# Pinned statistics and scalings in the later projections, and diagonal taps on TensorE in the last causal convolution

## The chip, the cores and the metric

The kernel runs on one core of a Trainium2 chip. The core has five engines with a queue each: TensorE (PE, matmuls), VectorE (DVE), ScalarE (ACT), GpSimd (POOL) and SyncE (SP), which only starts transfers here. The metric is the device time of one execution in microseconds (us); the median of three runs before the change is 3825.23 us. The profile is one execution of the same program, recorded by the hardware.

## The reference

The input is x of shape (4, 512, 128, 64): 4 batch entries, T = 512 time steps and D = 128 x 64 = 8192 features. All arithmetic is 32-bit float. Two layers follow each other.

Layer 0, for each batch entry:

1. Layer norm over D, then three projections to 64 columns, `k = xn @ Wk`, `v = xn @ Wv`, `r = sigmoid(xn @ Wr)`. A recurrence over time, `s = decay * s + k * v`, gives the states; `x = x + (r * states) @ Wo`.
2. Layer norm; a convolution with three taps along the 128 frequencies that mixes the 64 channels; GELU; added to x.
3. Layer norm; a *causal* depthwise convolution along time, three taps for each feature: `to[t] = w2 * xn[t] + w1 * xn[t-1] + w0 * xn[t-2] + bias`; layer norm of the result; added to x.
4. A feed-forward network, 64 channels to 256, GELU, back to 64; added to x.

Layer 1 is a spectral filter along time (moving average as trend, discrete Fourier transform of the rest, 128 modes mixed by complex matrices, inverse transform). The change does not touch it.

## The kernel before

**Tiling.** In layer 0 the 8192 features lie on the partitions in 64 chunks of 128, with the 512 time steps along the free axis. Chunks are handled in 32 pairs, so most tiles are 128 x 2 x 512. A layer norm over D is folded into the work: sums of x and of its squares come from matmuls against ones (`add_up`, L251), a few small operations give one factor and one offset for each time step, and `rows` spreads them over all partitions (L241 on TensorE, L285 on ScalarE).

**Stages**, for each batch entry b:

- `project(b)`: the three projections. Each pair of chunks needs the transposed x (`load_x`), a pair of weights, and for the first layer norm also x with time on the partitions (`xk`), from which VectorE takes `bn_stats` (L354). VectorE multiplies the weights by the norm's gain in place (L370), and TensorE accumulates over all chunks (L373).
- `scan(b)`: a short chain with the recurrence.
- `attend_and_convolve(b)`: `Wo` (L495), the addition to x (L497), normalising (L501), the frequency convolution (L516, L525, L530), GELU (L531), the residual (L533), squares (L536) and sums (L251) for the next norm.
- `convolve_time(b)`: the causal convolution. `normed` makes the normalised x in two VectorE operations (L569, L572); `tapped` makes one tap and the bias on ScalarE (L577) and adds the two others on VectorE (L581), chunk by chunk; GpSimd mends the first two time steps (L587) and stores (L588); ScalarE squares (L628). `convolve_ahead(b)` does 14 of the 32 pairs earlier, for b = 1 and 2.
- `open_feed(b)`, `feed_forward(b)`: for each pair the last norm and residual (L647, L648, L656, L659); for each chunk `widen` (L679, GELU L683), `narrow` (L690, residual L695) and `store` (transposes L704, copies L711 and L713, GpSimd's store L715).

**What sets the order.** TensorE's instructions stand in the order of the program. The list in `in_turn` pairs the stages: each entry gives two lanes of work, of which one step at a time is taken so that both advance by their shares. The entries that matter are feed-forward 0 beside projection 2, feed-forward 1 beside projection 3, and feed-forward 2 beside the causal convolution of b = 3, the last one. `begin` and `needed` hold a lane back until what it reads exists. On the other engines the framework's scheduler chooses the order from priorities and its own estimates, except for instructions marked by `tc.keep_in_program_order`, which keep the program's order among themselves and around them. Before the change, in projections 2 and 3 (`b > 1`), only the first of the two statistics of a pair is marked; the second and the scalings are placed by the scheduler.

**Buffers.** `xk` for `b > 1` lies alternately in the tags `x2` and `sq`, two buffers each; two pairs' weights share one `wx` buffer, of which there are two; `load_x` has three. `narrow` has a single PSUM bank, tag `p`, so L690 of a chunk waits for L695 of the chunk before. In the last convolution the sums lie in one of the two banks of the tile `a`, and the other is unused. SP's queue issues the loads of `project`, `normed` and `residual`; GpSimd's queue issues the stores.

Of the kernel before, what the change touches and what calls it, by code (L numbers as in the profile page):

```python
# [79 lines left out]
def layer0(ctx, tc, dram, x, xt, vecs, wkvr, wo, wdec, wconv, fbias, w1, fb1, w2, fb2, x4):  # L80
# [241 lines left out]
    def project(b):  # L322
# [5 lines left out]
        for i in range(NPR):  # L328
            first, last = i == 0, i == NPR - 1
            if unscanned[0]:  # L330

                wq, xk = two(fr, "x1")[:, :, 0 : 4 * S + 3], spare("z", SL)
            elif b == 1:

                both = spare("wx", 4 * S + SL)
                wq, xk = both[:, :, 0 : 4 * S], both[:, :, 4 * S :]
            else:

                xk = two(bk, "sq" if i % 2 else "x2")
                if i % 2 == 0:  # L340
                    pairs = spare("wx", 4 * S + SL).rearrange("p k n -> p (k n)")[:, 0 : 16 * S]
                    pairs = pairs.rearrange("p (c s) -> p c s", c=4)
                    nc.sync.dma_start(pairs, wkvr[2 * i : 2 * i + 4, :, 0 : 4 * S].rearrange("c p s -> p c s"))
                wq = pairs[:, i % 2 * 2 : i % 2 * 2 + 2, :]
            if b < 2:
                n = 4 * S + 2 * (b == 0)
                nc.sync.dma_start(wq[:, :, 0 : n], wkvr[2 * i : 2 * i + 2, :, 0 : n].rearrange("c p s -> p c s"))
            xp = load_x(b, i)
# [3 lines left out]
            )  # L352
            for t in range(2):
                stats = nc.vector.bn_stats(stt[:, h + t, s, :], xk[:, t, :])  # L354
                if b > 1 and t == 0:

                    tc.keep_in_program_order(stats)
            if b == 0:
# [9 lines left out]
            for j in range(2):  # L368
                w = wq[:, j, 0 : 3 * S]
                nc.vector.tensor_scalar_mul(w, w, vec[:, G1, 2 * i + j : 2 * i + j + 1])  # L370
# [108 lines left out]
    def attend_and_convolve(b):  # L479
        rst, rs, mrs = scanned.pop(b)  # L480
        rb, mb = yield from rows(of_a, rs, mrs, "rm")

        nc.vector.tensor_scalar(mb, mb, at_one[:, 1:2], at_one[:, 0:1], ALU.mult, ALU.add)
        st = ps_s.tile([P, SL], F32, tag="s", name="st")
        free_s[0] = False
# [58 lines left out]
        for i in range(2):  # L544
            scaled(i)
        for i in range(NPR + 3):
            if i < NPR:
                attend(i)
                yield 1.0
            if 1 < i < NPR + 2:  # L550
                convolve(i - 2)
                yield 5.0
            if i > 2:
                add_up(st, i - 3, *waiting.pop(i - 3), i == 3, i == NPR + 2)
                yield 1.0
        begin[attend_and_convolve], free_s[0] = b + 1, True
# [542 lines left out]
```

## Time and profile before

| what | value |
|---|---|
| median of three runs | 3825.23 us (3824.32 to 3826.63) |
| the profiled execution's own time | 3829.78 us |
| its span, first to last instruction | 3828.0 us |
| mean granted TensorE clock | 0.981 |
| VectorE taps, L581, x512 | 372.2 us busy, 0.74 us each |
| VectorE scalings, L370, x256 | 71.7 us busy, 0.31 to 0.32 us each |
| ScalarE tap and bias, L577, x256 | 200.1 us busy, 0.80 to 0.81 us each |

The page gives each engine's busy time as a share of the span and then groups of instructions by line: `L690 PE MATMUL pa<-mid,w_sb ... x2048` reads as line 690, TensorE, a matmul that writes tile `pa` from `mid` and `w_sb`, 2048 records. One 32-bit matmul leaves two records. Busy time of matmuls overlaps, because they are pipelined. "Idle before" is what the engine stood still just ahead of that group, with the instruction that ended it; idle time of an engine that is not the bound costs nothing. The stages follow each other: projection 0 to about 157 us; attention 0 beside projection 1 to 521; causal convolution 0 beside attention 1 to 810; feed-forward 0 beside projection 2 to 1264; convolution 1 beside attention 2 to 1510; feed-forward 1 beside projection 3 to 1927; convolution 2 beside attention 3 to 2174; feed-forward 2 beside convolution 3 to 2518; feed-forward 3 to 2831; layer 1 to the end.

### The profile page before, as it was taken

The page shows a single profiled execution, that of the slowest core. Times are in us where ns is not written, and L with a number is a line of the kernel's source. Part 1 is how long each engine was busy: PE and PEld are TensorE (multiplying, and loading weights), DVE is VectorE, ACT ScalarE, POOL GpSimd, SP SyncE. Part 2 cuts the span into 40 slices and gives each one's busy share as a digit, 9 for nine tenths or more (in the row PEclk, how much of TensorE's full clock was granted, in tenths as well). Part 3 has the DMA queues.
Part 4 walks back from the last instruction along what each step waited for, and adds up shares of the span by engine and source line. Part 5 has one row for each costly group of instructions (what it writes and reads, how often), then busy time and mean ns, then how long its engine had stood idle before and what let it go on. Part 6 is the DMA issues. An engine that isn't in the chain of part 4 may idle for free. (4 is left out here: it accounts for less than half of the span.)

```text
span 3828.0 us, 44882 instructions
## 1 busy us (share of the span) xinstructions
PE 3626.8 (95%) x15945; PEld 1344.1 (35%) x15945; DVE 2680.8 (70%) x3498; ACT 1762.2 (46%) x2491; POOL 510.8 (13%) x782
## 2 busy tenths in 40 slices
PE   9999999989899899999989989999989999999999
PEld 4433322233333223333322323333322843327533
DVE  4455569975667796677789699855558268892677
ACT  0022346645556565556756578867754210142100
POOL 0000012210011221011121121100013001121001
PEclk9999999999999999999989999999999999999999
DMA  9867657786775687777568677645559468994687
GB/s 311 267 210 247 217 171 254 262 276 228 250 250 195 215 281 270 261 262 278 203 233 284 215 247 256 218 155 176 187 197 283 145 215 295 313 307 145 200 289 271
DMA packets 429175, 912.80 MB, mean 238 GB/s; under 512 B 33240, under 2 KB 83608, under 8 KB 424856
## 3 DMA queue, kind: packets, MB, share of 16 engines
q1 hardware_dynamic: 351024, 636.87, 50.2%
q0 software_dynamic: 75776, 271.62, 20.4%
q8 instruction: 127, 2.08, 0.2%
q10 hardware_dynamic: 2152, 1.45, 0.1%
q14 instruction: 96, 0.79, 0.1%
HBM read 641.31 MB, written 268.50 MB: 238 GB/s over the span
## 5 line engine op out<-in xcount | busy, mean ns | idle before, releaser
L690 PE MATMUL pa<-mid,w_sb 128*64 128x512 f32 x2048 | 500.6, 610 | 56.5 <-DVE x4t L695 56.4
L683 ACT ACTIVATE mid<-m,fb_sb 128x1024 f32<-128x1024 f32 x256 | 284.9, 1113 | 264.4 <-PE m L679 264.1
L695 DVE SCALAR_TENSOR_TENSOR x4t<-pa,fb_sb,x 128x512 f32<-128x512 f32 x252 | 187.4, 744 | 225.1 <-PE pa L690 225.1
L679 PE MATMUL m<-x,w_sb 64*128 64x512 f32 x1008 | 289.4, 647 | 1.1 <-DVE x L659 0.7
L683 ACT ACTIVATE mid<-c,fb_sb 128x1024 f32<-128x1024 f32 x256 | 283.1, 1106 | 1.4 <-PE c L679 1.4
L679 PE MATMUL c<-x,w_sb 64*128 64x512 f32 x1008 | 264.1, 597 | 9.8 <-ACT mid L683 9.8
L690 PEld LDWEIGHTS pa<-mid,w_sb 128*64 128x64 f32 x2048 | 125.2, 137 | 401.4 <-issue 216.4
L373 PE MATMUL a<-xp,wx 128*128 128x512 f32 x512 | 243.0, 601 | 0.5 <-DVE me L268 0.5
L967 PE MATMUL b<-xin,avg_sb 128*128 128x512 f32 x512 | 230.8, 593 | 3.3 <-DVE xin L973 3.3
L944 ACT COPY two<-a 128x512 f32<-128x512 f32 x64 | 37.5, 585 | 425.2 <-PE a L939 425.2
L973 DVE TENSOR_TENSOR xin<-b,pm 128x512 f32<-128x512 f32 x256 | 158.9, 682 | 96.6 <-PE b L970 81.7
L536 ACT ACTIVATE sq<-x 128x1024 f32<-128x1024 f32 x128 | 135.0, 1055 | 179.8 <-DVE x L533 178.5
L581 DVE SCALAR_TENSOR_TENSOR to<-kd,vec,to 128x510 f32<-128x510 f32 (+1 forms) x272 | 196.8, 741 | 16.7 <-ACT to L577 11.0
L656 ACT ACTIVATE kd<-kd,vec 128x512 f32<-128x512 f32 x256 | 193.4, 809 | 4.1 <-DVE kd L648 4.1
L849 DVE COPY xf<-b 128x256 f32<-128x256 f32 x128 | 54.3, 424 | 185.0 <-PE b L913 173.3
L704 PEld LDWEIGHTS pt<-ident,x4t 128*128 128x128 f32 x1024 | 107.7, 141 | 208.5 <-ACT mid L683 141.2
L251 PE MATMUL st<-x,ones 128*32 128x512 f32 x512 | 168.3, 604 | 12.2 <-DVE x L533 12.1
L581 DVE SCALAR_TENSOR_TENSOR z<-x,vec,z 128x511 f32<-128x511 f32 x240 | 175.4, 743 | 5.2 <-ACT z L577 2.3
L870 DVE TENSOR_TENSOR uv<-xin 128x1024 f32<-128x1024 f32 x128 | 154.9, 1228 | 33.0 <-PE a L879 16.4
L495 PE MATMUL a<-rst,wo_sb 64*128 64x512 f32 x512 | 149.9, 660 | 28.7 <-DVE x L497 26.0
L497 DVE TENSOR_TENSOR x<-a,xp 128x1024 f32<-128x1024 f32 x128 | 155.9, 1218 | 27.0 <-PE a L495 24.3
L704 PE MATMUL pt<-ident,x4t 128*128 128x128 f32 x1024 | 168.7, 288 | 1.5 <-ACT ob L711 1.5
(241 smaller groups left out, 6513.4 us busy)
## 6 DMA issues: line engine op xcount, KB each, us to landing
xp<-in_xt SPq DMA_DIRECT2D x256, 512.0 KB
xin<-x SPq DMA_DIRECT2D x128, 1024.0 KB
kh<-to SPq DMA_DIRECT2D x156, 512.0 KB
x<-x POOLq DMA_DIRECT2D x128, 512.0 KB, 4.7
kx<-x SPq DMA_DIRECT2D x128, 512.0 KB
x<-ob POOLq DMA_DIRECT2D x64, 1024.0 KB, 6.1
out<-xin POOLq DMA_DIRECT2D x64, 1024.0 KB, 7.2
x<-x SPq DMA_DIRECT2D x96, 512.0 KB
```

The lines of the kernel that those rows point to most:

```text
L251: nc.tensor.matmul(st[32 * q : 32 * q + 32, :], lhsT=ones, rhs=src[:, j, :], start=first, stop=last,)
L373: nc.tensor.matmul(pa[:, k, :], lhsT=wq[:, j, k * P : (k + 1) * P], rhs=xp[:, j, :], start=first and j == 0, stop=last and j == 1,)
L497: nc.vector.tensor_tensor(x1, at, xp, ALU.add)
L581: tap = nc.vector.scalar_tensor_tensor(to[:, j, k:], xr[:, j, : SL - k], vec[:, w, c], to[:, j, k:], ALU.mult, ALU.add)
L656: tc.keep_in_program_order(nc.scalar.activation(d[:, j, :], d[:, j, :], AF.Identity, bias=vec[:, B4, c], scale=vec[:, G4, c]))
L679: nc.tensor.matmul(pm[:, h, :], lhsT=w1_sb[hs, m * P : (m + 1) * P], rhs=x3[hs, :], start=True, stop=True)
L683: nc.scalar.activation(mid, pm, AF.Gelu_apprx_tanh, bias=fb1_sb[:, m : m + 1])
L690: nc.tensor.matmul(pa[h * H : (h + 1) * H, :], lhsT=w2_sb[:, m, :], rhs=mid[:, h, :], start=(m == 0), stop=(m == 1),)
L695: nc.vector.scalar_tensor_tensor(x4t, pa, fb2_sb, x3s[c // 2][:, c % 2, :], ALU.add, ALU.add)
L704: nc.tensor.transpose(pt[:, t, :], x4t[:, t * P : (t + 1) * P], ident)
L967: nc.tensor.matmul(po[j], lhsT=avg_sb[:, j, :], rhs=xin[:, j, :], start=True, stop=False)
L973: nc.vector.tensor_tensor(by_n(xin[:, j, :]), by_n(po[j]), by_c(pm[j % 2][:, j // 2, :]), ALU.add)
```

## The change

It has three parts.

1. **Projections 2 and 3** (`project`, `b > 1`). Both statistics of a pair and both scalings are marked to keep the program's order. In the program the load of `xk` for pair i is issued at step i, and its statistics are taken at step i + 2; the weights are loaded for the two pairs after the current ones; `load_x` runs one pair ahead. The order within a step is: loads, the statistics of pair i - 2, the scalings of pair i, the matmuls of pair i.
2. **Attention 1's start.** A lane can now yield `BLOCKED` from inside a stage. Instead of waiting for the end of attention 0, attention 1 makes its rows at once (in buffers of their own, `rm4`) and may take its first three steps while attention 0's last ones are still under way. The PSUM bank for its sums is taken only at its fourth step.
3. **The last causal convolution** (`tapped` with `left`). In every other pair the second chunk gets all three taps on TensorE: GpSimd multiplies the identity by the three tap weights of the chunk, which gives three diagonal 128 x 128 matrices; three matmuls of 512, 511 and 510 columns add up in the unused bank of `a`; ScalarE adds the bias while it copies to SBUF. There are 16 such chunks of the 64. They need none of the two VectorE taps.

```diff
@@ -325,36 +325,60 @@
         if b == 0:
             psum_w = ps_p.tile([P, SL], F32, tag="p", name="psum_w")
         stt = rowp.tile([P, NT, NS, 6], F32, tag="stt", name="stt")
-        for i in range(NPR):
-            first, last = i == 0, i == NPR - 1
-            if unscanned[0]:
-
-                wq, xk = two(fr, "x1")[:, :, 0 : 4 * S + 3], spare("z", SL)
-            elif b == 1:
-
-                both = spare("wx", 4 * S + SL)
-                wq, xk = both[:, :, 0 : 4 * S], both[:, :, 4 * S :]
-            else:
-
-                xk = two(bk, "sq" if i % 2 else "x2")
-                if i % 2 == 0:
-                    pairs = spare("wx", 4 * S + SL).rearrange("p k n -> p (k n)")[:, 0 : 16 * S]
-                    pairs = pairs.rearrange("p (c s) -> p c s", c=4)
-                    nc.sync.dma_start(pairs, wkvr[2 * i : 2 * i + 4, :, 0 : 4 * S].rearrange("c p s -> p c s"))
-                wq = pairs[:, i % 2 * 2 : i % 2 * 2 + 2, :]
-            if b < 2:
-                n = 4 * S + 2 * (b == 0)
-                nc.sync.dma_start(wq[:, :, 0 : n], wkvr[2 * i : 2 * i + 2, :, 0 : n].rearrange("c p s -> p c s"))
-            xp = load_x(b, i)
+        def token_major(i, xk):
             s, h = i // 2, i % 2 * 2
             nc.sync.dma_start(
                 xk, x[b, h * P : (h + 2) * P, s * SL : (s + 1) * SL].rearrange("(t p) d -> p t d", p=P)
             )
+            return xk
+
+        def statistics(i, xk):
+            s, h = i // 2, i % 2 * 2
             for t in range(2):
                 stats = nc.vector.bn_stats(stt[:, h + t, s, :], xk[:, t, :])
-                if b > 1 and t == 0:
+                if b > 1:
 
                     tc.keep_in_program_order(stats)
+
+        def weights(i):
+
+            if i < NPR:
+                w = spare("wx", 4 * S + SL).rearrange("p k n -> p (k n)")[:, 0 : 16 * S]
+                w = w.rearrange("p (c s) -> p c s", c=4)
+                nc.sync.dma_start(w, wkvr[2 * i : 2 * i + 4, :, 0 : 4 * S].rearrange("c p s -> p c s"))
+                for k in range(2):
+                    ws[i + k] = w[:, 2 * k : 2 * k + 2, :]
+
+        ws, xps, xks = {}, {}, {}
+        if b > 1:
+            weights(0)
+            xps[0] = load_x(b, 0)
+        for i in range(NPR):
+            first, last = i == 0, i == NPR - 1
+            if b > 1:
+
+
+                xks[i] = token_major(i, two(bk, "sq" if i % 2 else "x2"))
+                if i % 2 == 0:
+                    weights(i + 2)
+                if not last:
+                    xps[i + 1] = load_x(b, i + 1)
+                wq, xp = ws.pop(i), xps.pop(i)
+                for k in (i - 2, NPR - 2, NPR - 1) if last else (i - 2,):
+                    if k in xks:
+                        statistics(k, xks.pop(k))
+            else:
+                if unscanned[0]:
+
+                    wq, xk = two(fr, "x1")[:, :, 0 : 4 * S + 3], spare("z", SL)
+                else:
+
+                    both = spare("wx", 4 * S + SL)
+                    wq, xk = both[:, :, 0 : 4 * S], both[:, :, 4 * S :]
+                n = 4 * S + 2 * (b == 0)
+                nc.sync.dma_start(wq[:, :, 0 : n], wkvr[2 * i : 2 * i + 2, :, 0 : n].rearrange("c p s -> p c s"))
+                xp = load_x(b, i)
+                statistics(i, token_major(i, xk))
             if b == 0:
                 nc.gpsimd.memset(wq[:, :, n:], 1.0)
                 for j in range(2):
@@ -367,7 +391,9 @@
                     )
             for j in range(2):
                 w = wq[:, j, 0 : 3 * S]
-                nc.vector.tensor_scalar_mul(w, w, vec[:, G1, 2 * i + j : 2 * i + j + 1])
+                scaled = nc.vector.tensor_scalar_mul(w, w, vec[:, G1, 2 * i + j : 2 * i + j + 1])
+                if b > 1:
+                    tc.keep_in_program_order(scaled)
             for j in range(2):
                 for k in range(2):
                     nc.tensor.matmul(
@@ -478,11 +504,9 @@
 
     def attend_and_convolve(b):
         rst, rs, mrs = scanned.pop(b)
-        rb, mb = yield from rows(of_a, rs, mrs, "rm")
+        rb, mb = yield from rows(of_a, rs, mrs, "rm4" if b == 1 else "rm")
 
         nc.vector.tensor_scalar(mb, mb, at_one[:, 1:2], at_one[:, 0:1], ALU.mult, ALU.add)
-        st = ps_s.tile([P, SL], F32, tag="s", name="st")
-        free_s[0] = False
         x1s, zs, ws, waiting = {}, {}, {}, {}
 
         def attend(i):
@@ -541,18 +565,26 @@
                 scaled(i + 2)
             waiting[i] = x2, sq2
 
-        for i in range(2):
-            scaled(i)
         for i in range(NPR + 3):
+
+            while begin[attend_and_convolve] < b + (min(i, 3) - 3) / 4:
+                yield BLOCKED
+            if i < 2:
+                scaled(i)
             if i < NPR:
                 attend(i)
                 yield 1.0
             if 1 < i < NPR + 2:
                 convolve(i - 2)
                 yield 5.0
+            if i == 3:
+                st = ps_s.tile([P, SL], F32, tag="s", name="st")
+                free_s[0] = False
             if i > 2:
                 add_up(st, i - 3, *waiting.pop(i - 3), i == 3, i == NPR + 2)
                 yield 1.0
+            if b == 0 and i >= NPR and i < NPR + 2:
+                begin[attend_and_convolve] = b + (0.25 if i == NPR else 0.75)
         begin[attend_and_convolve], free_s[0] = b + 1, True
         mean3, sq3 = yield from finish(st, of_a, 3)
         carried[b] = moments(mean3, sq3, 3)
@@ -571,9 +603,24 @@
             tc.keep_in_program_order(first)
         nc.vector.tensor_tensor(xr, xr, pair_of(mb), ALU.subtract)
 
-    def tapped(b, i, xr, to, pinned=False):
+    def tapped(b, i, xr, to, pinned=False, left=None):
+
         for j in range(2):
             c = slice(2 * i + j, 2 * i + j + 1)
+            if j == 1 and left is not None:
+                taps = fr.tile([P, 2, P + H], F32, tag="wcs", name="taps").rearrange("p k n -> p (k n)")
+                taps = taps.rearrange("p (k n) -> p k n", k=3)
+                nc.gpsimd.tensor_tensor(
+                    taps, ident.unsqueeze(1).to_broadcast([P, 3, P]),
+                    vec[:, W0 : W2 + 1, c].to_broadcast([P, 3, P]), ALU.mult,
+                )
+                for k in range(3):
+                    nc.tensor.matmul(
+                        left[:, k:], lhsT=taps[:, 2 - k, :], rhs=xr[:, j, : SL - k], start=k == 0, stop=k == 2,
+                        skip_group_check=True,
+                    )
+                nc.scalar.activation(to[:, j, :], left, AF.Identity, bias=tb_all[:, c])
+                continue
             nc.scalar.activation(
                 to[:, j, :], xr[:, j, :], AF.Identity, bias=tb_all[:, c], scale=vec[:, W2, c]
             )
@@ -607,7 +654,11 @@
             rb, mb = ahead.pop(b)
         else:
             rb, mb = yield from rows(bank, *moment, "rm" if b == B - 1 else "rm3")
-        st = bank()
+        if b == B - 1:
+            both = two(ps_a, "a")
+            st, left = both[:, 0, :], both[:, 1, :]
+        else:
+            st, left = bank(), None
         waiting, added = [], 0
         n = NPR - made
         for k in range(n + 2):
@@ -624,7 +675,7 @@
                     sq = bk.tile([P, 2, SL], F32, tag="sq4", name="sq4", bufs=2)
 
                 normed(b, made + k, x2, xr, rb, mb, made > 0 and k < 4)
-                tapped(b, made + k, xr, to)
+                tapped(b, made + k, xr, to, left=left if k % 2 else None)
                 nc.scalar.activation(sq, to, AF.Square)
                 waiting.append((k, to, sq))
                 i = k * made // n
@@ -740,11 +791,12 @@
 
 
     CHAIN = 6.0
+    BLOCKED = -1.0
 
     def run(b, stages):
         for stage, share in stages:
             for weight in stage(b):
-                yield weight * share / whole[stage]
+                yield BLOCKED if weight == BLOCKED else weight * share / whole[stage]
 
     def in_turn(leads, *pairs):
         at, running = [0.0, 0.0], [None, None]
@@ -754,10 +806,12 @@
             b, *stages = pairs[n][k]
             if running[k] is None:
                 first = stages[0][0]
-                if first in needed and b not in needed[first] or begin.get(first, b) < b:
+                if first in needed and b not in needed[first]:
                     return False
                 running[k] = run(b, stages)
             share = next(running[k], None)
+            if share == BLOCKED:
+                return False
             if share is None:
                 running[k] = None
                 at[k] = n + 1.0
```

## The prediction

> **What bounds the kernel now.** I read the page's engine totals first, then busy times by stretch, then the waits and the order of time inside two stretches. The stretches, by busy time of each engine (start and end in us, then each engine's busy us and count, the granted clock, the DMA share and GB/s):
>
> ```profile
> PE 3626.8 (95%) x15945; PEld 1344.1 (35%) x15945; DVE 2680.8 (70%) x3498; ACT 1762.2 (46%) x2491; POOL 510.8 (13%) x782
> ...
> 902.50:1173.30 270.80, 247.54 (x961) 88.93 (x960) 180.27 (x242) 149.22 (x201) 25.47 (x30) 1.00 0.73 249
> 1644.90:1864.80 219.90, 219.28 (x865) 80.75 (x864) 161.36 (x213) 133.28 (x181) 22.86 (x27) 1.00 0.78 271
> 2190.00:2470.00 280.00, 245.91 (x1192) 81.93 (x1192) 272.89 (x310) 233.79 (x310) 58.94 (x75) 0.98 0.72 242
> ```
>
> TensorE is the bound almost everywhere. The first stretch (feed-forward 0 beside projection 2) leaves it idle for 23 us. The second (feed-forward 1 beside projection 3) leaves it nothing: 9 equal cycles of four chunks take 219.9 us, 24.4 us each. The first stretch holds 10 such cycles, 27.1 us each. The third (feed-forward 2 beside the last causal convolution) is VectorE's: 272.9 of 280 us. Its waits, and those of the first stretch (who waited for whom, us in total, times, longest):
>
> ```profile
> DVE stt L354 <- DMA sq<-in_x: 54.8, 9, 7.0
> DVE stt L354 <- DMA x<-in_x: 27.6, 9, 3.2
> ...
> PE pa L690 <- DVE x4t L695: 32.8, 26, 3.9
> ```
>
> The first two lines are VectorE held up by the statistics' loads, in the first stretch; the third is TensorE waiting for VectorE, in the last. In order of time (start, us, line):
>
> ```profile
> 1003.77 0.68 DVE L354 BATCH_NORM_STATS2 stt<-sq 128x6 f32<-128x512 f32 x1
> 1011.45 0.69 DVE L354 BATCH_NORM_STATS2 stt<-sq 128x6 f32<-128x512 f32 x1 [7.00 <-DMA sq<-in_x]
> 1012.06 0.73 DVE L695 SCALAR_TENSOR_TENSOR x4t<-pa,fb_sb,x 128x512 f32<-128x512 f32 x1
> 1012.71 1.22 DVE L569 TENSOR_TENSOR x<-x,rm 128x1024 f32<-128x1024 f32 x1
> 1012.85 1.94 PE L690 MATMUL pa<-mid,w_sb 128*64 128x512 f32 x8 [1.78 <-DVE x4t L695]
> ...
> 1715.30 1.94 PE L690 MATMUL pa<-mid,w_sb 128*64 128x512 f32 x8
> 1717.17 0.66 PE L704 MATMUL pt<-ident,x4t 128*128 128x128 f32 x4
> 1717.29 0.75 DVE L695 SCALAR_TENSOR_TENSOR x4t<-pa,fb_sb,x 128x512 f32<-128x512 f32 x1 [3.06 <-PE pa L690]
> 1717.66 1.88 PE L373 MATMUL a<-xp,wx 128*128 128x512 f32 x4
> ```
>
> A statistic waits 7 us for a load that could start only when the statistic before it (1003.77) freed the buffer; the residual L695 queues behind it, and TensorE stands 1.78 us. Below, in cycle 2, the order that matters: narrow matmuls L690, transposes L704 0.49 us long, then the projection's matmuls L373. L695 starts only 0.12 us after the transposes, because it needs the end of L690.
>
> **What the skill says.** TensorE: Matmul & The Clock Gate, "Step-by-step: what each phase is for": matmuls stay in program order, only weight loads are pulled ahead. Its specification table gives the other engines strict first-in-first-out queues. The trace agrees: L690 at 1012.85 holds all behind it, and L695 stands behind the late statistic. Perfetto Trace Analysis, "Identifying the Most-Contended Engine", warns that matmul busy time is no measure of the roofline; so I use start-to-start steps.
>
> **Part 1, projections 2 and 3.** The loads move ahead: weights by two pairs, the transposed x by one, and the statistics run two pairs after their load. So each load is issued a cycle or so before its use, nothing new can block in SP's queue, and VectorE's DMA waits (54.8 + 27.6 = 82 us in the first stretch) should go. But all statistics and scalings are now pinned in program order. In the built program VectorE's order before was, per four chunks, residual, taps, four scalings in one go, drawn one to two pairs ahead, and L373 waited for no scaling. After, each pair reads: L695, statistic, statistic, scaling, scaling; and on TensorE the first L373 of the pair stands right behind L690 and the transposes. So it must wait for L695 (which needs that very L690), two statistics and one scaling. Loads that waited cost VectorE slack; this wait is TensorE's own.
>
> Steps from start to start in the traces above: L690 1.87, L704 0.49, L373 1.80, L679 0.96 and 0.95: 6.07 a chunk, 24.3 a cycle. VectorE: L695 0.66, statistic 0.61, scaling 0.31 to its end (0.23 to the next), 1024-wide operations 1.14 (1.25 when the next reads the result), taps 0.66. From VectorE's end to the matmul 0.06, and 0.1 more because the weights load after it (estimate from projection 0, where such pairs are 0.53 instead of 0.43 apart).
>
> Cycle in stretch 1, t=0 at the transposes. One pair has the short chain: 0.12 + 0.66 + 1.22 + 0.31 + 0.16 = 2.47 against 0.49 due: 1.98 us stall. For the other, VectorE is still busy with the normalising, residual and tap work that stands between: 0.12 + L695 0.66 + five 1024-wide 5.8 + two taps 1.32, then L695 0.66, 1.22, 0.31, 0.16: 10.25. TensorE would be there at 6.07 + 0.49 = 6.56: 3.7 us stall. The cycle is 24.3 + 5.7 = 29.95, against 27.1 now.
>
> Cycle in stretch 2: two pairs' statistics and scalings come in two bursts, behind two residuals, N (L569), X (L659), n (L572): 0.12 + 0.66 + 3.4 + 1.22 + 0.31 + 0.16 = 5.87 against 0.49: 5.4 us stall for one pair; the other's weights are ready. 24.3 + 5.4 = 29.7 against 24.4 now.
>
> Sum by the built order. Projection 2: four early pairs at 2.0 = 8; 10 cycles x 2.8 = 28; a half cycle 3.7 and a last pair behind six statistics (2.0 + 4 x 0.61 = 4.4) = 8: +44. Projection 3: four early 8, one cycle of the first kind 5.7, nine of the second 48.6, the last with four more statistics 7.8: 70, less some 5 us of stalls by late loads that go: +65. If VectorE reached each scaling by the time the transposes end, the cost would be nothing; the cover needed is a scaling ahead of L695, and the built order has none.
>
> **Part 2, attention 1 begins in attention 0's tail.** Its two row spreads and first matmuls move before the last sums. Around 500 to 550 us TensorE waits 7.6 us in pieces for rows, x and sums; I take -3 (0 to -5).
>
> **Part 3, taps on TensorE.** Removed: 32 VectorE taps x 0.74 = 23.7 us; 16 ScalarE scalings become copies with bias (0.80 before; evictions of this size take 0.59: no cost). Added: 48 matmuls of 128x512, two records 0.43 apart each: 0.86 x 48 = 41 us of TensorE; 16 diagonals of 384 columns on GpSimd. No trace shows those; GPSIMD Engine Reference, "3.1 Elementwise", states about 2.6 cycles an element: an estimate of 0.8 us, plus the 0.7 to 0.9 that even a 4-wide one takes here: 1.5. GpSimd builds them three pairs ahead, so TensorE shouldn't wait; the following square on ScalarE may come 0.5 us later. Queued behind that square are ScalarE's GELUs: 0 to 0.7 us a time, 16 times. The normalised x stands well ahead of the matmul in VectorE's order. In 2190 to 2470 TensorE does 48 chunks x 4.36 (the alone stage's step: 240 us for 55) + 28 sums x 1.0 = 237 us, to the 246 that show as busy. Plus 41: 279 to 288, plus 5 to 15 of stalls, against 280. From -1 to +23; I take +8. VectorE's 249 of 288 no longer binds.
>
> Total: 44 + 65 - 3 + 8 = +114. The profiled execution took 3829.78 (span 3828.0 and 1.8 around it), 4.6 over the median 3825.23; so 3944 profiled, **3939 us** as median.
>
> **Rivals.** (a) Short waits only: VectorE catches up and every affected pair costs 2.0. Projection 2: early 8, ten cycles at 28.3 (+12), tail 7: +27. Projection 3: 8, ten cycles +40, tail 2, less 5: +45. With +5: 3902. Against it: nothing in VectorE's order can overtake. (b) The diagonal path is worse: the square and GELU queue costs 2 us in each of 16 pairs, +32: 3971. For it: four engines in one chain there; against it: diagonals are ready early. (c) Faster: scalings are never late, and the DMA waits were the true cost: stretch 1 falls to 24.4 a cycle, 10 x 2.7 = -27, seam -3, taps 0: 3795. It decides when the mean wait of the 64 pairs stays under (27 + 3)/64 = 0.47 us; the shortest chain alone is 1.98. (d) Nothing measurable: gains of part 1 meet part 3's loss, 3825; it needs the same as (c).
>
> **Numbers.** Main 0.70, (a) 0.13, (b) 0.11, (c) 0.04, (d) 0.02. Its own range, with the taps at -1 to +23 and a tenth of part 1's 109 either way, is 3919 to 3965. To leave no more than 2 in 10 out I take 3892 (a, with the taps at -1) to 3974. A change under 0.2% (7.6 us) can't be told from none here: faster 0.04, same 0.02, slower 0.94.
>
> **What would show it.** Right: L373 idle before some 42 of 64 pairs with the scaling (L370 before) as releaser, 2 to 5.4 us each, 73 + 70 = 143 us by the sums above (57 + 16 and 70); four-chunk cycles near 30 us in both projections; no statistic waiting for a load; the last convolution's stage with VectorE near 86% and about as long as now. Wrong: L373 without such waits, because matmul and scaling stand otherwise than I read; or a last stage grown by over 25 us, with TensorE waiting for GpSimd or ScalarE.

## The result and the profile after

The changed kernel takes **4021.2 us** (median of 4 runs, 4016.38 to 4029.38), the kernel before, run beside it, 3824.78 us: ratio 1.052, 95% interval 1.0496 to 1.0543. That is 196 us slower, where +114 (3939 us) was forecast, and outside the range of 3892 to 3974. The direction was right, the size wrong.

The profiled execution took 4029.38 us (span 4027.6). From the page of the changed kernel, the engine totals and the group of the projection's matmuls, L399; below them the same group on the page of the kernel before, L373. After the bar come busy time (us), mean of one record (ns), idle time just ahead of the group, and what ended most of it:

```profile
PE 3731.0 (93%) x16041; PEld 1378.9 (34%) x16041; DVE 2672.6 (66%) x3466; ACT 1763.5 (44%) x2491; POOL 528.5 (13%) x798
...
L399 PE MATMUL a<-xp,wx 128*128 128x512 f32 x512 | 292.6, 704 | 148.5 <-DVE wx L394 141.9
...
L373 PE MATMUL a<-xp,wx 128*128 128x512 f32 x512 | 243.0, 601 | 0.5 <-DVE me L268 0.5
```

Two things are new: 141.9 us of waiting for the scaling (L394), and matmul records that take 704 ns instead of 601. The forecast had the first and not the second.

Busy time by stretch of the changed kernel (columns as in the prediction). The first two lines are the same stretches of time as there; the third is the stage of the last convolution, found by its own start and end:

```profile
902.50:1173.30 270.80, 227.75 (x816) 81.81 (x816) 151.05 (x200) 123.76 (x167) 20.38 (x24) 0.93 0.60 210
1644.90:1864.80 219.90, 186.26 (x696) 68.32 (x692) 125.60 (x163) 108.02 (x147) 16.74 (x20) 0.93 0.62 213
...
2335.90:2742.60 406.70, 374.06 (x1688) 132.50 (x1683) 318.25 (x338) 295.31 (x393) 80.65 (x96) 0.97 0.62 210
```

Beside both projections every engine does less per us than before, and the column of the granted clock, 1.00 in both before, is 0.93. Stage by stage, from where the stage before ends to where this one ends in the two profiled executions: feed-forward 0 with projection 2, 460.0 us before and 529.2 after (+69); feed-forward 1 with projection 3, 418.9 and 512.5 (+94); the last convolution, 374.0 and 406.7 (+33).

Waits of the changed kernel, beside projection 2 (850 to 1330 us; VectorE's, then TensorE's) and beside projection 3 (1618 to 2086 us; who waited for whom, us, times, longest):

```profile
DVE x4t L746 <- PE pa L741: 200.4, 47, 8.7
...
PE a L399 <- DVE wx L394: 66.0, 26, 4.0
...
PE a L399 <- DVE wx L394: 65.1, 16, 7.5
```

VectorE no longer waits for any load there (before, 82 us for the statistics' loads in the first stretch alone). It waits for L741 now: TensorE is late, and TensorE is late because L399 waits for VectorE. In order of time, TensorE first, then VectorE (start, us, instruction, idle before and its releaser):

```profile
1103.65 1.98 PE L399 MATMUL a<-xp,wx 128*128 128x512 f32 x4 [1.68 <-DVE wx L394]
1105.56 1.13 PE L730 MATMUL m<-x,w_sb 64*128 64x512 f32 x4
...
1115.44 0.66 PE L755 MATMUL pt<-ident,x4t 128*128 128x128 f32 x4
1119.59 3.78 PE L399 MATMUL a<-xp,wx 128*128 128x512 f32 x4 [3.49 <-DVE wx L394]
1123.30 2.08 PE L730 MATMUL m<-x,w_sb 64*128 64x512 f32 x4
...
1117.38 0.74 DVE L746 SCALAR_TENSOR_TENSOR x4t<-pa,fb_sb,x 128x512 f32<-128x512 f32 x1
1118.04 1.28 DVE L338 BATCH_NORM_STATS2 stt<-x 128x6 f32<-128x512 f32 x2
1119.23 0.53 DVE L394 TENSOR_SCALAR wx<-wx,vec 128x192 f32<-128x192 f32 x2
```

The forecast's chain is there: residual L746, two statistics, scaling, and then the matmul. Look at what follows each stall. `L399 ... x4` is one chunk: two matmuls, four records. (A transpose, L755, leaves one record.) After 1.68 us of standing still these two matmuls take 1.91 us to the next instruction. After 3.49 us they take 3.71, and the widen matmuls behind them 1.87 instead of 0.96: half rate, with records 0.85 us apart instead of 0.43. Over the 42 waits of L399 for the scaling in the two stretches above, worked out from start to start (the excess is over 1.81 + 0.96 + 0.95 us):

| stall ahead of L399 | count | mean L399 step | excess in all, L399 and widen |
|---|---|---|---|
| 1.68 us | 19 | 1.91 us | 2 us, 0.1 a time |
| 3.49 us, once 4.05 (mean 3.53) | 13 | 3.43 us | 29 us |
| 5.08 us, once 7.46 (mean 5.32) | 10 | 3.63 us | 22 us |

Two more waits, of 4.45 us each, stand near the starts of the projections ahead of eight records, which take 6.50 and 6.69 us; behind a third one, of 1.88 us, eight records take 3.54. The two of 4.45 us so add another 6 us. In all 25 long stalls are paid twice: some 57 us of matmuls at half rate stand behind them.

### The profile page after: what moved, and what is told of

Read it like the earlier page. It is cut to its first block, busy times and chain, and to the rows that moved or that the text cites. A ratio compares the mean times of both kernels' runs of the same rounds, so it can differ in the third digit from the quotient of the medians.

```text
span 4027.6 us, 44970 instructions
## 1 busy us (share of the span) xinstructions
PE 3731.0 (93%) x16041; PEld 1378.9 (34%) x16041; DVE 2672.6 (66%) x3466; ACT 1763.5 (44%) x2491; POOL 528.5 (13%) x798
## 5 line engine op out<-in xcount | busy, mean ns | idle before, releaser
L746 DVE SCALAR_TENSOR_TENSOR x4t<-pa,fb_sb,x 128x512 f32<-128x512 f32 x252 | 188.5, 748 | 565.6 <-PE pa L741 565.6
L741 PE MATMUL pa<-mid,w_sb 128*64 128x512 f32 x2048 | 498.3, 607 | 20.2 <-DVE x4t L746 20.2
L399 PE MATMUL a<-xp,wx 128*128 128x512 f32 x512 | 292.6, 704 | 148.5 <-DVE wx L394 141.9
L730 PE MATMUL m<-x,w_sb 64*128 64x512 f32 x1008 | 298.5, 665 | 6.3 <-ACT mid L734 6.3
L741 PEld LDWEIGHTS pa<-mid,w_sb 128*64 128x64 f32 x2048 | 124.7, 136 | 359.8 <-issue 246.6
L998 ACT COPY two<-a 128x512 f32<-128x512 f32 x64 | 37.5, 586 | 424.5 <-PE a L993 424.5
L399 PEld LDWEIGHTS a<-xp,wx 128*128 128x128 f32 x512 | 101.3, 218 | 248.8 <-DVE wx L394 154.7
L755 PEld LDWEIGHTS pt<-ident,x4t 128*128 128x128 f32 x1024 | 107.5, 141 | 208.0 <-ACT mid L734 156.6
L755 PE MATMUL pt<-ident,x4t 128*128 128x128 f32 x1024 | 168.4, 287 | 1.5 <-ACT ob L762 1.5
```

Of the source, the lines that this page charges most:

```text
L399: nc.tensor.matmul(pa[:, k, :], lhsT=wq[:, j, k * P : (k + 1) * P], rhs=xp[:, j, :], start=first and j == 0, stop=last and j == 1,)
L730: nc.tensor.matmul(pm[:, h, :], lhsT=w1_sb[hs, m * P : (m + 1) * P], rhs=x3[hs, :], start=True, stop=True)
L741: nc.tensor.matmul(pa[h * H : (h + 1) * H, :], lhsT=w2_sb[:, m, :], rhs=mid[:, h, :], start=(m == 0), stop=(m == 1),)
L746: nc.vector.scalar_tensor_tensor(x4t, pa, fb2_sb, x3s[c // 2][:, c % 2, :], ALU.add, ALU.add)
L755: nc.tensor.transpose(pt[:, t, :], x4t[:, t * P : (t + 1) * P], ident)
```

## The experiments

The theory after this reading: the pinned scaling behind the residual is the whole loss of the projections, by waiting and by half rate after long stalls; the taps lose because TensorE, not VectorE, bounds the last convolution's stage. Each expectation names what is set against it; theory A in the first four is this one. All ratios are to the kernel before, run on the same chip.

### One part at a time

The later projections alone (part 1), that is the hunks of the diff in `project`:

```diff
-                if b > 1 and t == 0:
+                if b > 1:
...
+                scaled = nc.vector.tensor_scalar_mul(w, w, vec[:, G1, 2 * i + j : 2 * i + j + 1])
+                if b > 1:
+                    tc.keep_in_program_order(scaled)
```

> Part 1 alone (projections 2 and 3 as changed, attention and taps as before). Theory A, pinned scalings: L373 waits for its scaling behind the residual, 142 us of waiting in the changed kernel, and the matmuls after the long ones of these waits ran at half speed, some 55 us more, less some 30 us of stalls of before that go: +163 us, 3988 (3978 to 3998). Theory B, the three parts make each other worse (taps or attention 1's start slow the projections): well under that, under 3960, with the missing rest in no other single part.

Measured: 3992.58 us, ratio 1.0434 (1.0412 to 1.0455), +166 us.

Attention 1's early start alone (part 2), the hunks in `attend_and_convolve`, `run` and `in_turn`:

```diff
-        rb, mb = yield from rows(of_a, rs, mrs, "rm")
+        rb, mb = yield from rows(of_a, rs, mrs, "rm4" if b == 1 else "rm")
...
+            while begin[attend_and_convolve] < b + (min(i, 3) - 3) / 4:
+                yield BLOCKED
```

> Part 2 alone (attention 1 begins in attention 0's tail). In the changed kernel attention 0 ended 11 us later and attention 1 only 3 us later than before, so theory A gives this part -8 to 0: 3817 to 3826. Theory B, the earlier first steps disturb attention 0's tail: +5 to +12, 3830 to 3837.

Measured: 3826.36 us, ratio 1.0 (0.9985 to 1.0014). Nothing that can be told from no change.

The taps alone (part 3), the hunks in `tapped` and `convolve_time`:

```diff
-                tapped(b, made + k, xr, to)
+                tapped(b, made + k, xr, to, left=left if k % 2 else None)
```

> Part 3 alone (taps by diagonal matrices in the last causal convolution). The stage took 33 us longer in the changed kernel. Theory A, it is the part's own work (41 us of matmuls for 17 us of TensorE's stalls removed): +33, 3858 (3848 to 3868). Theory B, the stage suffered from what the projections left behind: under +15, 3840 or less.

Measured: 3865.13 us, ratio 1.0098 (1.0078 to 1.0118), +37.5 us.

The three add up to 204 us against 196; the difference is within their intervals, of some 8 us each. Part 1 is four fifths of it.

### The pin on the scalings

All of the change, but the scalings left to the scheduler:

```diff
-                scaled = nc.vector.tensor_scalar_mul(w, w, vec[:, G1, 2 * i + j : 2 * i + j + 1])
-                if b > 1:
-                    tc.keep_in_program_order(scaled)
+                nc.vector.tensor_scalar_mul(w, w, vec[:, G1, 2 * i + j : 2 * i + j + 1])
```

> The changed kernel, only the scalings are no longer pinned; the loads stay ahead and the statistics two pairs behind, pinned. Theory A, the pin on the scalings is the whole loss of part 1: VectorE draws them ahead again, L373 waits for none, the cycle beside projection 2 falls from 27.1 before to 24.4 us, 10 cycles, -27; with +33 of taps: 3831 (3820 to 3842). Theory B, the loads moved ahead or the late statistics are the loss: 3950 or more, with the stalls still there.

Measured: 3826.35 us, ratio 1.0 (0.9989 to 1.0011). Three lines carry the whole 196 us. And since the taps alone lose 37 us, something else in part 1 must win about as much. The same edit without the taps and without part 2:

> Later projections alone, with both statistics pinned and late and the loads ahead, but the scalings left to the scheduler. Theory (the scalings' pin is the loss, and late statistics with loads ahead are a gain that the whole change hides): level with the scalings one pair ahead, 3787 us, 3780 to 3797, with TensorE's waits for the residual in the second projection's stage down by some 20 us. Rival (the statistics' pin brings nothing; the lead of the scalings is what gained): 3825 us.

Measured: 3791.83 us, ratio 0.9918 (0.9898 to 0.9938): a gain of 31 us, hidden in the whole change. Of the kernel with only the statistics pinned, the busy times in the stretch 902.5 to 1173.3 us, and then TensorE's wait for the residual between 850 and 1210 us:

```profile
902.50:1173.30 270.80, 268.93 (x1074) 100.31 (x1074) 202.69 (x268) 165.86 (x225) 29.31 (x35) 1.00 0.77 269
```

```profile
PE pa L714 <- DVE x4t L719: 4.4, 4, 1.5
```

TensorE is busy for all but 2 us, where before it lost 23; the same wait was 17.4 us before. This is the forecast's rival (c), in the part of the change where it holds.

### Is it the stall or the half rate?

The changed kernel with long stalls filled by repeated transposes, just ahead of the waiting matmuls. The edit fills 23 of them, not 24 as the expectation says: thirteen with six times the transposes and ten with nine. The two of 4.45 us stay as they are.

```diff
+            again = 1
+            if b == 0 and (c % 4 == 0 and 8 <= c <= 48 or c == 50) or b == 1 and c == 8:
+                again = 6
+            elif b == 1 and c % 4 == 3 and 15 <= c <= 51:
+                again = 9
-            for t in range(NT):
+            for t in range(NT * again):
+                t = t % NT
```

> The changed kernel with the long stalls filled: just ahead of 24 projection steps that stall long, the four transposes of the pair before are repeated (6 times in all beside the second projection, 9 times beside the third), rewriting the same values. No wait is removed: the scaling still stands behind the residual. Theory (the stalls cost twice, once as waiting, once as matmuls at half rate after a stall of 3.5 us or more): the waiting before the projection matmuls shrinks only because TensorE is now busy in it, the mean of a projection matmul falls from 704 ns to about 600 to 620, and most of the 56 us of half-rate excess goes: 3960 to 3985 us. Rival (the matmuls are slow for another reason, the freshly scaled weights or contention with VectorE and the loads): mean stays at about 700 ns and the time at 4021 us or above.

Measured: 3977.43 us, ratio 1.0391 (1.0356 to 1.0425): 49 us less than the changed kernel by the ratios, 57 by the spans (3970.3 against 4027.6). From its page, and then its TensorE in order of time, where a stall of the kind shown above is filled with six times the four transposes:

```profile
L399 PE MATMUL a<-xp,wx 128*128 128x512 f32 x512 | 257.0, 629 | 85.2 <-DVE wx L394 78.6
...
L761 PE MATMUL pt<-ident,x4t 128*128 128x128 f32 x1604 | 231.6, 282 | 1.5 <-ACT ob L768 1.5
```

```profile
1093.94 2.84 PE L761 MATMUL pt<-ident,x4t 128*128 128x128 f32 x24
1098.09 1.98 PE L399 MATMUL a<-xp,wx 128*128 128x512 f32 x4 [1.31 <-DVE wx L394]
1100.00 1.13 PE L730 MATMUL m<-x,w_sb 64*128 64x512 f32 x4
```

The transposes' busy time rose from 168.4 to 231.6 us and the idle time ahead of L399 fell from 148.5 to 85.2: 63 us both. The weights are ready no sooner; TensorE only spends the time otherwise. Yet L399 is 36 us less busy, and behind 21 of the 23 filled stalls the step is 1.91 us again. Useless work made the kernel faster, so the half rate comes from the standing still, and not from the fresh weights or from other traffic. Where half rate is left, standing still is left too: 3.96 us of the longest stall, with a step of 3.61 us behind it; 1.87 us of another, with a step of 2.66; and the two unfilled ones of 4.45 us, with 6.35 and 6.40 us for their eight records.

The same question from the other side: later projections alone, with the scalings ahead of the statistics, which shortens every chain by two statistics.

```diff
-                for k in (i - 2, NPR - 2, NPR - 1) if last else (i - 2,):
-                    if k in xks:
-                        statistics(k, xks.pop(k))
...
                 if b > 1:
                     tc.keep_in_program_order(scaled)
+            for k in (i - 2, NPR - 2, NPR - 1) if last else (i - 2,):
+                if k in xks:
+                    statistics(k, xks.pop(k))
```

> Later projections alone, all pinned, with the scalings of a pair placed ahead of the statistics instead of behind. Two statistics of 0.61 us leave each of 43 chains: 52 us less waiting, some 88 us left before the projection matmuls. Theory (half rate only after stalls of about 3.5 us and more): the 14 stalls of 3.6 us fall to 2.4 and lose their 34 us of half rate, so 86 us in all: 3907 us, 3900 to 3922, with projection steps at 1.9 us after stalls of under 2.5 us. Rival (half rate goes with the time waited, at any length): steps after such stalls still slow by a third, 3919 us or more. If another instruction is late next, such as the residual: above 3940 us.

Measured: 3907.27 us, ratio 1.0222 (1.0198 to 1.0247), 81 us less by the ratios than part 1 with the statistics first; from the page and in order of time:

```profile
L399 PE MATMUL a<-xp,wx 128*128 128x512 f32 x512 | 265.3, 646 | 90.4 <-DVE wx L391 83.8
```

```profile
972.02 2.41 PE L399 MATMUL a<-xp,wx 128*128 128x512 f32 x4 [2.31 <-DVE wx L391]
974.36 2.08 PE L705 MATMUL m<-x,w_sb 64*128 64x512 f32 x4
...
1084.46 1.98 PE L399 MATMUL a<-xp,wx 128*128 128x512 f32 x4 [2.31 <-DVE wx L391]
1086.37 1.13 PE L705 MATMUL m<-x,w_sb 64*128 64x512 f32 x4
...
1722.50 3.78 PE L399 MATMUL a<-xp,wx 128*128 128x512 f32 x4 [3.90 <-DVE wx L391]
1726.22 1.89 PE L705 MATMUL m<-x,w_sb 64*128 64x512 f32 x4
```

The waiting fell by 58 us (141.8 to 83.8). The stalls of 3.5 us are 2.31 us now: behind 10 of 12 the step is 1.91 us; behind two (the first pair of lines is one) half rate costs some 1.7 us, L399 and widen together. Behind the 10 stalls of 3.90 us half rate is still there, 22 us of it. Of two stalls of 3.26 us near the starts of the projections one is followed by it and one is not. So the length of a stall alone does not decide; the last section comes back to this.

### Scaling one pair ahead

Part 1 with everything still pinned, but the weights of pair i + 1 scaled in step i (and pair 0 ahead of the loop):

```diff
+            for j in range(2):
+                w = ws[0][:, j, 0 : 3 * S]
+                tc.keep_in_program_order(nc.vector.tensor_scalar_mul(w, w, vec[:, G1, j : j + 1]))
...
-            for j in range(2):
-                w = wq[:, j, 0 : 3 * S]
-                scaled = nc.vector.tensor_scalar_mul(w, w, vec[:, G1, 2 * i + j : 2 * i + j + 1])
+            for k in (i + 1,) if b > 1 else (i,):
+                for j in range(2) if k < NPR else ():
+                    w = (ws[k] if b > 1 else wq)[:, j, 0 : 3 * S]
+                    scaled = nc.vector.tensor_scalar_mul(w, w, vec[:, G1, 2 * k + j : 2 * k + j + 1])
```

> Later projections alone (no diagonal taps, attention as before), scalings still pinned in program order but drawn one pair ahead: in step i the weights of pair i+1 are scaled, and pair 0 is scaled ahead of the loop. Theory (the whole loss of the projections is that the pair's own scaling stands behind the residual of the step before): the waits of the projection matmuls on the scaling fall from some 135 us to under 15, the half rate goes with them, and the kernel is level with the one before or a little ahead, since the statistics are pinned late: 3795 us, 3785 to 3830. Rival (pinning the statistics, or any fixed order on VectorE, costs by itself): above 3850 us.

Measured: **3787.49 us**, ratio 0.989 (0.9868 to 0.9912): 42 us faster than the kernel before and the fastest that was run; the version with free scalings (0.9918) is not clearly behind it. In order of time (VectorE, then TensorE), and its stretch:

```profile
1004.75 0.74 DVE L725 SCALAR_TENSOR_TENSOR x4t<-pa,fb_sb,x 128x512 f32<-128x512 f32 x1
1005.41 1.27 DVE L338 BATCH_NORM_STATS2 stt<-x 128x6 f32<-128x512 f32 x2
1006.60 0.53 DVE L398 TENSOR_SCALAR wx<-wx,vec 128x192 f32<-128x192 f32 x2
...
1008.90 0.66 PE L734 MATMUL pt<-ident,x4t 128*128 128x128 f32 x4
1009.39 1.88 PE L403 MATMUL a<-xp,wx 128*128 128x512 f32 x4
```

```profile
902.50:1173.30 270.80, 270.80 (x1070) 99.51 (x1066) 206.42 (x277) 166.11 (x224) 29.31 (x35) 1.00 0.78 275
```

The order on VectorE is the same, residual, statistics, scaling. Only the pair that the scaling belongs to is another, and TensorE has no idle time left in this stretch. Pinning as such costs nothing here.

### Where the gain of part 1 comes from

The kernel before, with the statistics taken two pairs after their load and nothing else changed:

```diff
+            xks[i] = xk
-            for t in range(2):
-                stats = nc.vector.bn_stats(stt[:, h + t, s, :], xk[:, t, :])
-                if b > 1 and t == 0:
-                    tc.keep_in_program_order(stats)
+            for k in (i,) if b < 2 else (i - 2, NPR - 2, NPR - 1) if last else (i - 2,):
+                if k in xks:
+                    s, h, xk = k // 2, k % 2 * 2, xks.pop(k)
+                    for t in range(2):
+                        stats = nc.vector.bn_stats(stt[:, h + t, s, :], xk[:, t, :])
+                        if b > 1 and t == 0:
+                            tc.keep_in_program_order(stats)
```

> The kernel before with one edit: in projections 2 and 3 the statistics of a pair are taken two pairs after its load, nothing else moves, no more is pinned. Theory (the statistics waiting for their loads cost the second projection's stage its idle time): most of the 38 us gain, 3787 to 3800 us, and VectorE waits less than 20 us for those loads instead of 82. Rival (the weights and x loaded ahead bring the gain): 3815 to 3826 us.

Measured: 3824.89 us, ratio 1.0004 (0.9993 to 1.0016). A miss: no gain, and between 850 and 1210 us VectorE waits for these loads as long as before (99.5 us; before, 98.0). In order of time on VectorE:

```profile
1007.27 0.68 DVE L359 BATCH_NORM_STATS2 stt<-x 128x6 f32<-128x512 f32 x1
1007.87 0.76 DVE L374 TENSOR_SCALAR wx<-wx,vec 128x192 f32<-128x192 f32 x3
1011.58 0.69 DVE L359 BATCH_NORM_STATS2 stt<-x 128x6 f32<-128x512 f32 x1 [2.95 <-DMA x<-in_x]
```

A statistic at 1007.27 frees the buffer, and the next one on VectorE already wants what is loaded into it (the load is issued at 1007.98). Two things that this kernel lacks and the gaining ones have are the pin on the second statistic and the loads issued ahead. With the pin both statistics of a pair stand together, as at 1005.41 above; which of the two brings the gain was not tried apart.

### The last convolution's stage

Which engine bounds it? First the kernel before without the 32 VectorE taps:

```diff
-            for k, w in ((1, W1), (2, W0)):
+            for k, w in ((1, W1), (2, W0)) if not (bare and j == 1) else ():
...
-                tapped(b, made + k, xr, to)
+                tapped(b, made + k, xr, to, bare=b == B - 1 and k % 2 == 1)
```

> The kernel before with the two VectorE taps of the same 16 chunks left out and nothing put in their place: two of three taps of these chunks are not computed. 32 taps of 0.74 us, 23.7 us of VectorE, go. The prediction's reading (VectorE bounds the last convolution's stage): 18 to 24 us less, 3801 to 3808 us. Rival (TensorE bounds the stage, VectorE's work is mostly cover): 0 to 8 us less, 3817 to 3826 us.

Measured: 3820.24 us, ratio 0.9992 (0.9983 to 1.0002). 23.7 us of VectorE are worth 3 us. Then the taps alone, with one matmul of three (the expectation counts records, two a matmul):

```diff
-                for k in range(3):
+                for k in range(1):
```

> Diagonal taps alone, with one of the three tap matmuls per half chunk: two of the three taps of those 16 chunks are left out. 64 of 96 matmuls go, 30 us of TensorE; copy, build and fix-ups stay. Theory (the stage is TensorE's, and the loss is its own added work): 27 us less than with all three, 3838 us, 3833 to 3845. Rival (the longer way over the copy on ScalarE and the fix-up on GpSimd delays the GELU): 0 to 8 us less, 3857 to 3865.

Measured: 3838.61 us, ratio 1.0026 (1.0017 to 1.0036), 27 us less than with three. And the taps alone, with a single build of the diagonals:

```diff
+                if not diag:
+                    taps = fr.tile([P, 2, P + H], F32, tag="wcs", name="taps").rearrange("p k n -> p (k n)")
...
+                    diag.append(taps)
+                taps = diag[0]
```

> Diagonal taps alone, with one diagonal built once and used by all 16 chunks: 15 chunks get another chunk's tap weights, so that part of the computation is changed. 15 diagonal builds of 1.5 us leave GpSimd. Rival (the builds delay GpSimd's fix-ups, and with them square and GELU): about 3857 us or less. Theory (TensorE's own added matmuls, 45 us, are the loss, and GpSimd's builds lie beside other work): 3865 us, 3861 to 3869.

Measured: 3849.29 us, ratio 1.0059 (1.0040 to 1.0079), 15 us less than with 16 builds. That goes against the theory as it was put: the builds do hold something. The stage in the profiled executions (its length, then TensorE's and VectorE's busy time, in us):

| kernel | stage | TensorE busy | TensorE not busy | VectorE busy |
|---|---|---|---|---|
| before | 374.0 | 331.0 | 43.0 | 328.7 |
| taps left out | 368.9 | 332.5 | 36.4 | 309.6 |
| one matmul of three | 382.3 | 347.4 | 34.9 | 314.5 |
| one build for all | 398.3 | 373.4 | 24.9 | 311.2 |
| taps on TensorE (part 3) | 408.5 | 376.0 | 32.5 | 318.4 |

The stage follows TensorE's busy time much more closely than VectorE's: 28.6 us of TensorE between the third and the last row are 26.2 us of the stage, 19.1 us of VectorE between the first two are 5.1. Of the 10.2 us between the last two rows 7.6 are TensorE's idle time; the waits say whose. First the stage before and its largest wait of TensorE, then the stage with 16 builds (who waited for whom, us, times, longest), and then with one:

```profile
2173.30:2547.30 374.00, 330.96 (x1592) 115.91 (x1587) 328.66 (x369) 295.94 (x392) 65.53 (x83) 0.97 0.67 228
PE pa L690 <- DVE x4t L695: 34.7, 29, 3.9
```

```profile
PE pa L709 <- DVE x4t L714: 19.6, 14, 2.6
...
ACT sq L647 <- POOL z L602: 23.0, 16, 2.4
...
PE m L698 <- ACT mid L702: 5.8, 6, 1.7
```

```profile
ACT sq L652 <- POOL z L607: 7.3, 16, 0.8
```

The build stands on GpSimd's queue ahead of the fix-up (z L602), the square waits for the fix-up, the GELU waits behind the square, and the widen matmuls wait for the GELU: 5.8 us, which are gone with a single build. It accounts for that much of the 15 us; the stages differ by 10 us, and the rest lies in other stages, which the edit doesn't touch.

## Why the prediction was wrong

**Right: the chain and the waits of the projections.** VectorE's order after the change was read off correctly, and with it the wait of L399 for the scaling behind a residual. Forecast were 42 pairs and 143 us, measured 45 waits and 141.9. By projection: 73 forecast and 70.5 measured, 70 and 71.4 (the 66.0 and 65.1 shown above leave out three waits near the starts of the projections). The stalls of 1.98, 3.7 and 5.4 us measured 1.68, 3.49 and 5.08; the forecast counted from the 0.49 us step of the transposes, the profile from their end at 0.66, so 0.17 us of the 0.2 to 0.3 us between them is only the way of counting. That VectorE's waits for loads go was right as well, and their worth (cycles of 27.1 instead of 24.3 us, about 30 us) agrees with the 31 us that pinned statistics with free scalings gain.

**Wrong: "the cycle is 24.3 + 5.7 = 29.95", "24.3 + 5.4 = 29.7".** Both sums price a stall at its own length and keep all other steps as they were. Measured from long stall to long stall, the cycles take 32.2 us in projection 2 (958.52 to 1248.57, nine cycles) and 31.9 in projection 3 (1737.88 to 1993.05, eight). The missing 2.2 us a cycle are the two matmuls behind the long stall, up to 3.7 instead of 1.8 us, with part of the widen matmuls behind them. In all that is some 57 us, and it is what part 1's forecast of 109 lacks against the measured 166. The term that the sum puts at nothing is the rate of TensorE after a stall. The step was a matter of looking up, too. The Trainium skill, TensorE: Matmul & The Clock Gate, "What's actually happening", states that TensorE falls to half its clock after an idle window of about 3.4 us and needs about as long a busy stretch to come back; its section "HAM oscillation — how this bites in real kernels" describes a kernel that pays this at every step of a loop. Here the records do go to half rate, but not by a limit of 3.4 us on the stall: 3.49 us gave half rate 12 times of 12, 1.68 us beside the projections never, and 2.31 us twice of 12. The page was used for the matmuls' order and not for this.

**Wrong: "the third stretch ... is VectorE's: 272.9 of 280 us".** A busy engine needn't be the bound: 23.7 us less of VectorE gave 3 us. TensorE bounds that stage with 331 of 374 us busy. Its idle time comes mostly in pieces tied to the residual (34.7 us of waits), and extra matmuls at other places filled them only in part: 19.6 us were left with part 3, and new waits came in.

**Wrong: "Plus 41: 279 to 288 ... against 280".** Three things were in this. The matmuls were sized right, 45 us busy for 41 forecast. The base of 237 us, work without stalls, let them run in the idle time: of 43.0 us of it, part 3 filled 10.5. And the diagonals, sized right at 1.5 us (the group's mean is 1393 ns), were taken as hidden: "so TensorE shouldn't wait". The square was delayed by up to 2.4 us rather than 0.5. So +8 became +37.5, above the forecast's own -1 to +23. Rival (b), with 32 us on top of the +8, came nearest in size, but by luck: its queue is the smaller part of the loss. The forecast's own sign of being wrong, a last stage grown by over 25 us, came true with +33.

**Part 2**, forecast at -3, can't be told from nothing.

**The range** missed because every slower case in it shared the first fault, stalls priced at their length, and all but (b) laid the taps' matmuls into idle time. Part by part the forecast lacks 57 us in the projections, 29 in the taps and 3 in part 2. These add up to 89 where the whole lacks 82, as the parts add up to 204 for 196.

## What to carry to other kernels

Where a change adds waits to TensorE, ask for their length, not only their sum: here, beside the projections, a stall of 1.68 us cost itself, one of 3.49 us or more cost some 2.2 us on top. If such a stall can't go, filling it with harmless transposes won back 49 us, but drawing the late operand one pair ahead won some 205 on part 1 alone (3992.58 to 3787.49). Where an operation is pinned behind another, look at whose data it makes; the same fixed order on VectorE cost 166 us with this pair's weights and gained 42 with the next pair's. And before work is moved off an engine because it is 97% busy, leave the work out once and see what the time does.

## What was not expected of the hardware

Half rate doesn't always begin with the first matmul after the stall. Behind equal stalls of 3.90 us the same two matmuls took 2.50, 3.05 or 3.78 us; where they took 2.50, the widen matmuls behind them took 1.86 us instead of 0.96 and carried the rest. Nor does the excess grow with the stall: it is 2.2 us a time behind 3.53 us and 2.2 behind 5.32.

One thing explains both, and the two cases behind 2.31 us: half rate begins and ends on a fixed grid in time. It can be worked out record by record from the trace with the scalings ahead of the statistics. Behind its last nine stalls of 3.90 us half rate ends at 1697.20, 1727.92, 1758.64 and so on to 1942.96 us, 30.72 us apart each time, though the stalls are 30.17 to 31.09 us apart. The 12 ends behind its stalls of 2.31 and 3.90 us all lie whole steps of 3.413 us apart, to 0.02 us (30.72 is nine steps), and so do the six places where half rate begins only after the matmuls have started. In the changed kernel's trace 23 ends lie on such a grid too, to 0.12 us. What counts is how much of a stall falls into one step of the grid. In that trace with the scalings first, the two stalls of 2.31 us that were paid twice have 1.85 and 2.05 us in one step; the ten others have at most 1.83, cut in two by a point of the grid, and the harmless stall of 3.26 us is cut into 1.90 and 1.36. In the changed kernel each of the 23 has at least 2.10 us in one step, and 1.68 us can't reach 1.85. So the border lay near 1.9 us of 3.413 here, and a longer stall makes half rate more certain rather than dearer. This is read from the traces afterwards; no run was made to test it.

The border is that of this stage. In layer 1 of the kernel before, matmuls ran at half rate behind a stall of 1.64 us, where the same ones otherwise take 1.94 us; why is open:

```profile
3328.83 1.94 PE L879 MATMUL a<-uv,dftd_sb 128*64 128x512 f32 x8
...
3334.43 3.32 PE L879 MATMUL a<-uv,dftd_sb 128*64 128x512 f32 x8 [1.64 <-DVE uv L870]
```
